# A two-layer graph network on one core: p turned by VectorE and the weights of a tile made in four operations

## The chip, the cores and the metric

The kernel runs on one core of a Trainium2 chip. A core has five engines that run beside each other and meet only at semaphores: TensorE (matrix multiplication; its weight loads are listed apart), VectorE, ScalarE and GpSimd (elementwise work; in the profile DVE, ACT and POOL), and SyncE (SP), which here only issues transfers. POOL issues transfers too. All transfers run on 16 DMA engines. Operands lie in SBUF, 128 partitions wide; matrix products arrive in PSUM, which TensorE writes and VectorE or ScalarE reads.

The metric is the device time of one execution in microseconds, the median of several runs.

## The reference

Sixteen graphs (B) of 1024 nodes (N) with 256 features (D) pass through two layers, each followed by a residual sum and a layer norm. `adj` holds 0 or 1.

Layer 0 takes scores e = leaky(h * a0 @ h^T), a sigmoid where `adj` is 1, and alpha @ h + bias. Layer 1 is an attention whose logits are a sum of a row's and a column's term:

```python
Hh = h @ W
s, d = Hh @ a_src, Hh @ a_dst
e = where(adj != 0, exp(-leaky_relu(s[:, None] + d[None, :], 0.2)), 0)
h_prime = (e @ Hh) / rowsum(e)
x = layernorm(x + elu(h_prime))
```

The exponential of the sum factors. With p = exp(-0.8 s) and q = exp(-0.8 d), and with exp(-0.2 d) put into Hh and what depends on the row alone cancelled by the division, a weight becomes min(p * q, adj): p runs along the columns of a tile (the rows i of the result), q along its partitions (the nodes j that are summed over).

## The kernel before

A batch is 8 tiles of 128 nodes. `adj` lies transposed, so a tile has the summed node j on the partitions and all 1024 rows i on the free axis, in bf16 (`adjs`, two halves of four tiles). The main loop runs over b = 1 to 15 and has three stages, each with a loop of eight steps. The order of the instructions is written out by hand: every engine takes its own in the order of the program, and each waits only for what it reads or overwrites.

1. Strips. For each tile jt of batch b: the scores on TensorE (L227), two tanh on ScalarE (L235, L236), their maximum on VectorE (L237), times `adj` into `al` (`finish`, L243), the diagonal on POOL (L253). The scores are symmetric, so only the upper half is computed: `dump` turns a strip in 32x32 blocks (L259) and stores it (`mir`), `gather` loads it as columns of the lower half of `al`, and `mask` (L274) finishes these. Between the strips TensorE makes Hh of the batch before (`project`, L405), and ScalarE takes from it exp(-0.2 d) (L413), p and q (L414) and Hh (L415). At step 6 `share_p` brings p to all partitions.
2. Sums of layer 0. For each tile t: eight products (L342), then bias and residual (L352), statistics (L295, L297) on VectorE. The weights of layer 1 of the batch before (`weights`, L449) stand among these: none at steps 0 and 1, tiles 0 and 1 at step 2, then 2, 3, 4, 5, and tiles 6 and 7 at step 7, each ahead of that step's L352.
3. Sums of layer 1 of the batch before. For each tile t: eight products of `es` with Hh (L456), which take the weights' tiles in the order 0 to 7; then division and ELU (L479, L480, L488, L489), residual (L494, L496), statistics; beside it x and x1 are turned for the next batch (L191, L381).

The last batch has no next one. Its p is spread without a transfer: TensorE transposes a column that is repeated 128 times (`spread_p`, L424) and ScalarE copies it (L425). Its weights are made while TensorE already multiplies: `weights` 0 before the division of the tile that closes batch 14, 1 to 3 after it, 4 to 7 in a loop over m in which each tile is used for four products at once.

p, before: `project` leaves p and q as pairs, p of tile t in column (t, 0) of `pqs` (three buffers). `share_p` has TensorE transpose the eight columns to 8 rows of 128 (L431), ScalarE copy them (L433), POOL store the 4 KB (L435), wait, and load them back onto all 128 partitions (L437). Both transfers stand in POOL's queue between the diagonals of tiles 6 and 7 (L253). The sums keep their results in three PSUM buffers (`ps_acc`); a transposed p takes one of `ps_t`.

Of the kernel before, what the change touches and what calls it, by code (L numbers as in the profile page):

```python
# [9 lines left out]
F32 = mybir.dt.float32  # L10
# [3 lines left out]
AF = mybir.ActivationFunctionType  # L14
ALU = mybir.AluOpType
# [3 lines left out]
P = 128  # L19
HALF = 512  # L20
BIG = 1.0e30
SLOPE = 0.2
SQ = 32
# [7 lines left out]
def one_kind_pass(  # L31
# [33 lines left out]
    nc = tc.nc  # L65
    B, N, D = x.shape
    NT = N // P
    ND = D // P
    HT = HALF // P
# [4 lines left out]
    const = ctx.enter_context(tc.tile_pool(name="const", bufs=1))  # L74
    four = ctx.enter_context(tc.tile_pool(name="four", bufs=4))
    one = ctx.enter_context(tc.tile_pool(name="one", bufs=1))
    two = ctx.enter_context(tc.tile_pool(name="two", bufs=2))
    dram = ctx.enter_context(tc.tile_pool(name="dram", bufs=2, space=bass.MemoryType.DRAM))
    small = ctx.enter_context(tc.tile_pool(name="small", bufs=3))
    ps_e = ctx.enter_context(tc.tile_pool(name="ps_e", bufs=3, space=PSUM))  # L80
    ps_t = ctx.enter_context(tc.tile_pool(name="ps_t", bufs=2, space=PSUM))
# [5 lines left out]
    xs, adjs = {}, {}  # L87
# [56 lines left out]
    ident = const.tile([P, P], F32, tag="ident", name="ident")  # L144
# [20 lines left out]
    pcol = ps_e.tile([P, HALF], F32, tag="e", name="pcol")[:, 0:ND]  # L165
    nc.tensor.transpose(pcol, arow, ident[0:ND, 0:ND])
    nc.scalar.copy(acol, pcol)
    power = const.tile([P, NT], F32, tag="power", name="power")
    nc.gpsimd.memset(power, -0.5)
    def make_Wx(c):  # L170
# [191 lines left out]
    x1Ts, Hs, pqs, p_bcs, es = {}, {}, {}, {}, {}  # L362
# [28 lines left out]
    def project(b, t):  # L391

        if t == 0:
            if b < B - 1:
                H = one.tile([P, NT, D + 1], F32, tag="H", name=f"H_{b}")
                Hs[b] = [H[:, m, :] for m in range(NT)]
            else:
                Hs[b] = []
                for g in range(2):
                    H = two.tile([P, HT, D + 1], F32, tag=f"adj{g}", name=f"H_{b}_{g}")  # L400
                    Hs[b] += [H[:, m, :] for m in range(HT)]
            pqs[b] = small.tile([P, NT, 2], F32, tag="pq", name=f"pq_{b}")
        pt = ps_acc.tile([P, D + 2], F32, tag="acc", name=f"pH_{b}_{t}")
        for c in range(ND):
            nc.tensor.matmul(  # L405
                pt,
                lhsT=x1Ts[b][:, c, ts(t, P)],
                rhs=Wx[:, c, :],
                start=(c == 0),
                stop=(c == ND - 1),  # L410
            )
        w = Hs[b][t][:, D : D + 1]
        nc.scalar.activation(w, pt[:, 1:2], AF.Exp, scale=-SLOPE)  # L413
        nc.scalar.activation(pqs[b][:, t, :], pt[:, 0:2], AF.Exp, scale=SLOPE - 1.0)  # L414
        nc.scalar.mul(Hs[b][t][:, 0:D], pt[:, 2:], w)  # L415

    def spread_p(b, g):

        if g == 0:
            p_bcs[b] = one.tile([P, N], F32, tag="p", name=f"p_{b}")  # L420
        pt = ps_t.tile([P, HT, P], F32, tag="t", name=f"pp_{b}_{g}")
        for t in range(HT):
            col = pqs[b][:, g * HT + t, 0:1]
            nc.tensor.transpose(pt[:, t, :], col.to_broadcast([P, P]), ident)  # L424
        nc.scalar.copy(p_bcs[b][:, ts(g, HALF)], pt.rearrange("p t q -> p (t q)"))  # L425

    def share_p(b):


        pt = ps_t.tile([P, HT, P], F32, tag="t", name=f"prow_{b}")[0:NT, 0, :]  # L430
        nc.tensor.transpose(pt, pqs[b][:, :, 0], ident)  # L431
        row = one.tile([NT, P], F32, tag="row", name=f"row_{b}")
        nc.scalar.copy(row, pt)  # L433
        p_row = dram.tile([N], F32, tag="p_row", name=f"p_row_{b}")
        nc.gpsimd.dma_start(p_row.rearrange("(t p) -> t p", p=P), row)  # L435
        p_bcs[b] = one.tile([P, N], F32, tag="p", name=f"p_{b}")
        nc.gpsimd.dma_start(p_bcs[b], p_row.partition_broadcast(P))  # L437

    def check_pq(b):
        near = small.tile([P, NT, 2], F32, tag="near", name=f"near_{b}")  # L440
        nc.vector.tensor_scalar(near, pqs[b], LOW, 1.0 / LOW, ALU.max, ALU.min)
        nc.vector.tensor_tensor(near, near, pqs[b], ALU.is_equal)
        nc.vector.tensor_reduce(fit[:, b : b + 1], near, AX.XY, ALU.min)

    def weights(b, m):

        if m == 0:
            es[b] = one.tile([P, NT, N], F32, tag="ew" if b < B - 1 else "al", name=f"e_{b}")
        nc.vector.scalar_tensor_tensor(  # L449
            es[b][:, m, :], p_bcs[b], pqs[b][:, m, 1:2], adjs[b, m // HT][:, m % HT, :], ALU.mult, ALU.min  # L450
        )

    hs, ys, y_of, mv1s, r1s = {}, {}, {}, {}, {}

# [108 lines left out]
    for b in range(1, B):  # L563
# [7 lines left out]
        for jt in range(NT):  # L571
            if jt == 4:
                mask(b, 0)
            strip(b, jt)
            if prev == 0 and jt < 2:
                scale0(0, HT + 2 * jt)
                scale0(0, HT + 2 * jt + 1)
            finish(b, jt)
            if jt < NT - 1:
                dump(b, jt)  # L580
            if prev == 0 and jt == 0:
                turn_x1(0, 0)
            if prev == 0 and jt == 2:
                transpose_x1(0)
            if jt >= 1:
                gather(b, jt - 1)
            for t in projects[jt]:
                project(prev, t)
            if jt == 6:
                share_p(prev)  # L590
            if jt >= 6:
                mask(b, jt - 5)
        check_pq(prev)
        if not last:
            load_x(b + 1, [nc.sync])
# [26 lines left out]
        for t in range(NT):  # L622
# [59 lines left out]
    for m in range(NT):  # L682
# [421 lines left out]
def kernel(  # L1104
# [69 lines left out]
```

## Time and profile before

The median is 1272.78 us (1272.75 to 1272.94, three runs).

| | us |
|---|---|
| the profiled execution's own time | 1273.82 |
| its span | 1271.7 |
| TensorE's matmuls busy | 1261.2 (99%) |
| weight loads (beside them) | 1025.7 (81%) |
| VectorE | 924.9 (73%) |
| ScalarE | 651.4 (51%) |
| GpSimd | 293.5 (23%) |
| L449, the weights, 128 x 1269 ns | 159.7 |
| L431, the transpose of p, 15 x 273 ns | 4.1 |
| VectorE's waits for p | 26.1 in 15 |

Times in the profile count from the start of the span. A line of the timeline gives start, duration, engine, line, operation, result and operands, number of instructions, and in brackets how long the engine had been idle and what ended that. Where a line stands for several instructions (x2), its duration runs from the first one's start to the last one's end. A line of the busy times by stretch gives the stretch, its length, then for PE, PEld, DVE, ACT and POOL the busy time and the number of instructions, TensorE's granted clock, the DMA engines' busy share and GB/s.

### The profile page before, as it was taken

How to read it: one execution, taken by the hardware profiler on the slowest of the kernel's cores; microseconds unless marked ns; L12 is line 12 of the kernel's file. 1: busy time of each engine (PE TensorE's matmuls, PEld its weight loads, DVE VectorE, ACT ScalarE, POOL GpSimd, SP SyncE). 2: the span in 40 equal slices, each digit the busy share in tenths (PEclk: the TensorE clock that was granted, in tenths of full speed). 3: DMA queues.
4: the chain of work that ended last, by engine and by line, in shares of the span. 5: the costliest groups of instructions: out<-in, count | busy, mean ns of one | idle time of the engine just before them, and what ended most of it. 6: DMA issues, size and time to landing. Idle time of an engine off the chain costs nothing.

```text
span 1271.7 us, 17514 instructions
## 1 busy us (share of the span) xinstructions
PE 1261.2 (99%) x5484; PEld 1025.7 (81%) x5484; DVE 924.9 (73%) x2017; ACT 651.4 (51%) x1469; POOL 293.5 (23%) x593
## 2 busy tenths in 40 slices
PE   9999999999999999999999999999999999999997
PEld 6788787887878878788787887878788787887886
DVE  5686867858678686786768868687686867868657
ACT  4644645456454564544645445454455645456434
POOL 2213231212312122121232212223112231212203
PEclk9999999999999999999999999999999999999999
DMA  9388595895949869497695966949579595895312
GB/s 219 67 174 143 103 188 96 176 181 101 194 88 180 168 117 200 77 183 154 130 194 92 182 133 139 209 83 182 117 168 188 95 190 97 174 181 103 99 34 69
DMA packets 603416, 180.24 MB, mean 142 GB/s; under 512 B 481722, under 2 KB 585652, under 8 KB 603316
## 3 DMA queue, kind: packets, MB, share of 16 engines
q1 hardware_dynamic: 581760, 135.85, 54.3%
q0 software_dynamic: 20864, 42.53, 18.6%
q8 instruction: 46, 0.75, 0.3%
q10 hardware_dynamic: 692, 0.66, 0.2%
q14 instruction: 54, 0.44, 0.1%
HBM read 151.91 MB, written 60.62 MB: 167 GB/s over the span
## 4 chain that ended last, share of the span: by engine, by line
PE 98%; DMA 1%; DVE 0%; ACT 0%; issue 0%; ACTq 0%; DVEq 0%
PE acc L342 35%; PE acc L456 35%; PE pe L227 19%; PE pH L405 9%; DMA x<-in_x 1%; PE pal L282 0%; PE prow L431 0%; PE pp L424 0%; ACT y L325 0%; ACT y_kept L325 0%; ACT L666 0%; PE px1T L388 0%; DVE y L494 0%; PE pxT L203 0%; ACTq L136 0%
## 5 line engine op out<-in xcount | busy, mean ns | idle before, releaser
L342 PE MATMUL acc<-x,al 128*128 128x256 f32 x2048 | 445.5, 379 | 0.0
L456 PE MATMUL acc<-H,e 128*128 128x257 f32 x2032 | 445.3, 380 | 0.0
L456 PEld LDWEIGHTS acc<-H,e 128*128 128x128 f32 x2032 | 384.8, 190 | 57.2 <-DVE e L449 0.6
L342 PEld LDWEIGHTS acc<-x,al 128*128 128x128 f32 x2048 | 387.7, 190 | 51.7
L227 PE MATMUL pe<-xa,xT 128*128 128x384 f32 (+1 forms) x720 | 250.9, 486 | 0.0
L227 PEld LDWEIGHTS pe<-xa,xT 128*128 128x128 f32 x720 | 132.7, 189 | 80.8 <-issue 43.1
L325 ACT ACTIVATE x<-x,mr,r 128x256 f32<-128x256 f32 x128 | 69.4, 592 | 227.8 <-POOL mr L321 227.8
L449 DVE SCALAR_TENSOR_TENSOR e<-p,pq,adj 128x1024 f32<-128x1024 f32 x128 | 159.7, 1269 | 29.2 <-DMA p<-p_row 26.1
L304 POOL TENSOR_SCALAR ve<-mv 128x4 f32<-128x4 f32 (+2 forms) x49 | 16.8, 343 | 657.0 <-DVE mv L297 652.9
L488 ACT ACTIVATE h<-acc,rinv 128x256 f32<-128x256 f32 x126 | 59.1, 469 | 203.4 <-DVE rinv L480 187.9
L235 ACT ACTIVATE tb<-pe 128x512 f32<-128x512 f32 (+1 forms) x192 | 94.1, 490 | 119.8 <-PE pe L227 94.6
L479 DVE TENSOR_SCALAR rinv<-acc 128x1 f32<-128x1 f32 x127 | 19.9, 157 | 161.2 <-PE acc L456 161.1
L237 DVE TENSOR_TENSOR tb<-tb,low 128x512 f32<-128x512 f32 (+1 forms) x192 | 103.3, 543 | 39.9 <-ACT low L236 39.8
L125 ACT ACTIVATE junk<-adj,minus 128x2048 bf16<-128x2048 bf16 x64 | 127.3, 1989 | 0.0
L405 PE MATMUL pH<-Wx,x1T 128*128 128x258 f32 x512 | 126.3, 381 | 0.0
L405 PEld LDWEIGHTS pH<-Wx,x1T 128*128 128x128 f32 x512 | 97.2, 190 | 35.8 <-issue 14.3
L253 POOL TENSOR_TENSOR al<-ident,al 128x128 f32<-128x128 f32 x128 | 67.0, 523 | 230.4 <-DVE al L243 229.9
L243 DVE SCALAR_TENSOR_TENSOR al<-tb,adj 128x512 f32<-128x512 f32 (+7 forms) x132 | 97.4, 739 | 5.3 <-DVE tb L237 0.4
L236 ACT ACTIVATE low<-pe 128x512 f32<-128x512 f32 (+1 forms) x192 | 93.2, 485 | 0.5 <-DVE tb L237 0.5
L274 DVE SCALAR_TENSOR_TENSOR al<-al,adj 128x512 f32<-128x512 f32 (+3 forms) x150 | 77.3, 539 | 19.7 <-DMA al<-mir 19.6
L352 DVE SCALAR_TENSOR_TENSOR x<-acc,bias_bc 128x256 f32<-128x256 f32 x128 | 53.7, 420 | 41.5 <-PE acc L342 41.5
L259 DVE STREAM_TRANSPOSE tb<-tb 128x896 f32<-128x896 f32 (+6 forms) x105 | 74.7, 712 | 3.6
(108 smaller groups left out, 950.1 us busy)
## 6 DMA issues: line engine op xcount, KB each, us to landing
adj<-in_adjT POOLq DMA_DIRECT2D x30, 1024.0 KB, 10.3
x_rows<-x SPq DMA_DIRECT2D x31, 512.0 KB, 4.6
x1T<-x_rows SPq DMA_DIRECT2D x248, 64.0 KB, 2.5
out<-y_kept SPq DMA_DIRECT2D x30, 512.0 KB, 6.8
x<-in_x SPq DMA_DIRECT2D x14, 1024.0 KB, 6.1
xT<-in_x SPq DMA_DIRECT2D x112, 128.0 KB, 4.7
p<-p_row POOLq DMA_DIRECT2D x15, 512.0 KB, 4.5
mir<-tb SPq DMA_DIRECT2D x60, 112.0 KB, 3.0
```

Of the source, the lines that this page charges most:

```text
L125: nc.scalar.activation(junk, rows, AF.Square, bias=minus1, scale=2.0, accum_out=chk[:, b * CHECKS + n : b * CHECKS + n + 1],)
L227: nc.tensor.matmul(pe[:, 0:w], lhsT=xTs[b][:, c, ts(jt, P)], rhs=xas[b][:, c, ds(jt * P + o, w)], start=(c == 0), stop=(c == ND - 1),)
L235: nc.scalar.activation(tb[:, ds(o, w)], pe[:, 0:w], AF.Tanh, scale=0.5)
L236: nc.scalar.activation(low[:, 0:w], pe[:, 0:w], AF.Tanh, scale=0.5 * SLOPE)
L237: nc.vector.tensor_tensor(tb[:, ds(o, w)], tb[:, ds(o, w)], low[:, 0:w], ALU.max)
L243: nc.vector.scalar_tensor_tensor(als[b][:, jt, c0:c1], tbs[b, jt][:, c0 - jt * P : c1 - jt * P], 1.0, adjs[b, jt // HT][:, jt % HT, c0:c1] ...
L259: nc.vector.transpose(tb, tb)
L274: nc.vector.scalar_tensor_tensor(v, v, 1.0, rows, ALU.add, ALU.mult)
L342: nc.tensor.matmul(acc, lhsT=als[b][:, jt, ts(t, P)], rhs=xs[b][:, jt, :], start=(jt == 0), stop=(jt == NT - 1),)
L405: nc.tensor.matmul(pt, lhsT=x1Ts[b][:, c, ts(t, P)], rhs=Wx[:, c, :], start=(c == 0), stop=(c == ND - 1),)
L449: nc.vector.scalar_tensor_tensor(es[b][:, m, :], p_bcs[b], pqs[b][:, m, 1:2], adjs[b, m // HT][:, m % HT, :], ALU.mult, ALU.min)
L456: nc.tensor.matmul(acc, lhsT=es[b][:, m, ts(t, P)], rhs=Hs[b][m], start=(m == 0), stop=(m == NT - 1),)
```

## The change

p and q are kept apart in one tile `pq_kept`, 128 x 32, cleared once: columns 0 to 7 hold p of the eight tiles, columns 8 to 15 q, the rest zeros. `share_p` turns it in one instruction on VectorE, which transposes each 32x32 block by itself: block i then has p of the nodes 32 i to 32 i + 31 of every tile in its first 8 rows. One DMA stores all 128 rows of 32 numbers (16 KB), and one loads of each of the four blocks its first 8 rows (four runs of 1 KB) onto all partitions. So p lies there as (i, t, j), where it was (t, i, j). The weights of a tile are made in four operations of 8 x 32 elements each, one for each i, whose result and `adj` have 32 neighbouring elements in each tile of columns.

`spread_p` of the last batch writes p in the new order with the same two copies. `check_pq` follows the new shape. Nothing else is moved.

```diff
+    pq_kept = const.tile([P, SQ], F32, tag="pq", name="pq_kept")
+    nc.gpsimd.memset(pq_kept, 0.0)
@@ project
-            pqs[b] = small.tile([P, NT, 2], F32, tag="pq", name=f"pq_{b}")
+            pqs[b] = pq_kept[:, 0 : 2 * NT].rearrange("p (k t) -> p k t", k=2)
-        nc.scalar.activation(pqs[b][:, t, :], pt[:, 0:2], AF.Exp, scale=SLOPE - 1.0)
+        nc.scalar.activation(pqs[b][:, :, t], pt[:, 0:2], AF.Exp, scale=SLOPE - 1.0)
@@ spread_p
-            p_bcs[b] = one.tile([P, N], F32, tag="p", name=f"p_{b}")
+            p_bcs[b] = one.tile([P, P // SQ, NT, SQ], F32, tag="p", name=f"p_{b}")
-            col = pqs[b][:, g * HT + t, 0:1]
+            col = pqs[b][:, 0, ds(g * HT + t, 1)]
-        nc.scalar.copy(p_bcs[b][:, ts(g, HALF)], pt.rearrange("p t q -> p (t q)"))
+        nc.scalar.copy(
+            p_bcs[b].rearrange("p i t j -> p t i j")[:, ts(g, HT), :, :],
+            pt.rearrange("p t (i j) -> p t i j", j=SQ),
+        )
@@ share_p
-        pt = ps_t.tile([P, HT, P], F32, tag="t", name=f"prow_{b}")[0:NT, 0, :]
-        nc.tensor.transpose(pt, pqs[b][:, :, 0], ident)
-        row = one.tile([NT, P], F32, tag="row", name=f"row_{b}")
-        nc.scalar.copy(row, pt)
-        p_row = dram.tile([N], F32, tag="p_row", name=f"p_row_{b}")
-        nc.gpsimd.dma_start(p_row.rearrange("(t p) -> t p", p=P), row)
-        p_bcs[b] = one.tile([P, N], F32, tag="p", name=f"p_{b}")
-        nc.gpsimd.dma_start(p_bcs[b], p_row.partition_broadcast(P))
+        pT = one.tile([P, SQ], F32, tag="pT", name=f"pT_{b}")
+        nc.vector.transpose(pT, pq_kept)
+        p_row = dram.tile([P // SQ, SQ, SQ], F32, tag="p_row", name=f"p_row_{b}")
+        nc.gpsimd.dma_start(p_row.rearrange("i t j -> (i t) j"), pT)
+        p_bcs[b] = one.tile([P, P // SQ, NT, SQ], F32, tag="p", name=f"p_{b}")
+        nc.gpsimd.dma_start(p_bcs[b], p_row[:, 0:NT, :].partition_broadcast(P))
@@ weights
-        nc.vector.scalar_tensor_tensor(
-            es[b][:, m, :], p_bcs[b], pqs[b][:, m, 1:2], adjs[b, m // HT][:, m % HT, :], ALU.mult, ALU.min
-        )
+        e = es[b][:, m, :].rearrange("p (t i j) -> p i t j", i=P // SQ, j=SQ)
+        rows = adjs[b, m // HT][:, m % HT, :].rearrange("p (t i j) -> p i t j", i=P // SQ, j=SQ)
+        for i in range(P // SQ):
+            nc.vector.scalar_tensor_tensor(
+                e[:, i], p_bcs[b][:, i], pqs[b][:, 1, m : m + 1], rows[:, i], ALU.mult, ALU.min
+            )
```

More of the change, by code (lines that the diff above doesn't have):

```diff
@@ L419, in spread_p @@
         if g == 0:
-            p_bcs[b] = one.tile([P, N], F32, tag="p", name=f"p_{b}")
+            p_bcs[b] = one.tile([P, P // SQ, NT, SQ], F32, tag="p", name=f"p_{b}")
         pt = ps_t.tile([P, HT, P], F32, tag="t", name=f"pp_{b}_{g}")
         for t in range(HT):
-            col = pqs[b][:, g * HT + t, 0:1]
+            col = pqs[b][:, 0, ds(g * HT + t, 1)]
             nc.tensor.transpose(pt[:, t, :], col.to_broadcast([P, P]), ident)
-        nc.scalar.copy(p_bcs[b][:, ts(g, HALF)], pt.rearrange("p t q -> p (t q)"))
+        nc.scalar.copy(
+            p_bcs[b].rearrange("p i t j -> p t i j")[:, ts(g, HT), :, :],
+            pt.rearrange("p t (i j) -> p t i j", j=SQ),
+        )
     def share_p(b):
-        pt = ps_t.tile([P, HT, P], F32, tag="t", name=f"prow_{b}")[0:NT, 0, :]
-        nc.tensor.transpose(pt, pqs[b][:, :, 0], ident)
-        row = one.tile([NT, P], F32, tag="row", name=f"row_{b}")
-        nc.scalar.copy(row, pt)
-        p_row = dram.tile([N], F32, tag="p_row", name=f"p_row_{b}")
-        nc.gpsimd.dma_start(p_row.rearrange("(t p) -> t p", p=P), row)
-        p_bcs[b] = one.tile([P, N], F32, tag="p", name=f"p_{b}")
-        nc.gpsimd.dma_start(p_bcs[b], p_row.partition_broadcast(P))
+        pT = one.tile([P, SQ], F32, tag="pT", name=f"pT_{b}")
[4 more added lines that the diff above has]
+        nc.gpsimd.dma_start(p_bcs[b], p_row[:, 0:NT, :].partition_broadcast(P))
     def check_pq(b):
-        near = small.tile([P, NT, 2], F32, tag="near", name=f"near_{b}")
+        near = small.tile([P, 2, NT], F32, tag="near", name=f"near_{b}")
         nc.vector.tensor_scalar(near, pqs[b], LOW, 1.0 / LOW, ALU.max, ALU.min)
```

## The prediction

> **What bounds the kernel now.** The page comes first, for who is full and what the chain that ended last is made of; then the busy time of one batch, cut into its three stages; then the instructions around the change in order of time; then the same at the end of the program, where the last batch has no next one to hide behind.
>
> ```profile
> span 1271.7 us, 17514 instructions
> PE 1261.2 (99%) x5484; PEld 1025.7 (81%) x5484; DVE 924.9 (73%) x2017; ACT 651.4 (51%) x1469; POOL 293.5 (23%) x593
> PE 98%; DMA 1%; DVE 0%; ACT 0%; issue 0%; ACTq 0%; DVEq 0%
> ...
> 624.83:652.46 27.63, 27.63 (x131) 24.34 (x129) 22.50 (x47) 9.79 (x20) 8.80 (x14) 1.00 0.95 174
> 652.46:680.30 27.84, 27.84 (x130) 24.25 (x128) 16.45 (x46) 14.89 (x27) 3.31 (x9) 1.00 0.82 163
> 602.26:624.83 22.57, 22.57 (x82) 14.87 (x81) 19.02 (x34) 15.76 (x48) 6.89 (x13) 1.00 0.56 100
> ```
>
> TensorE never rests, at full clock, in any stage. So only two things can move the time: instructions taken from TensorE, and moments at which it is made to wait. The stage to look at is the first of the three rows, the sums of layer 0, because the weights are made beside it: VectorE is busy 22.50 of 27.63 us there, and its results must be ready when TensorE comes to them.
>
> ```profile
> 624.27 0.27 PE L431 MATMUL prow<-ident,pq 128*8 128x128 f32 x1
> 624.38 0.61 PE L227 MATMUL pe<-xa,xT 128*128 128x128 f32 x4
> ...
> 626.50 0.46 POOL L253 TENSOR_TENSOR al<-ident,al 128x128 f32<-128x128 f32 x1 [0.82 <-DVE al L243]
> 626.89 0.64 POOL L435 DMA_DIRECT2D p_row<-row  x1
> 631.35 0.55 POOL L437 DMA_DIRECT2D p<-p_row  x1 [3.82 <-DMA p_row<-row]
> 636.30 2.48 DVE L449 SCALAR_TENSOR_TENSOR e<-p,pq,adj 128x1024 f32<-128x1024 f32 x2 [2.54 <-DMA p<-p_row]
> 649.21 0.42 DVE L352 SCALAR_TENSOR_TENSOR x<-acc,bias_bc 128x256 f32<-128x256 f32 x1 [1.16 <-PE acc L342]
> 650.23 2.45 DVE L449 SCALAR_TENSOR_TENSOR e<-p,pq,adj 128x1024 f32<-128x1024 f32 x2
> 652.46 3.86 PE L456 MATMUL acc<-H,e 128*128 128x257 f32 x17
> ...
> 1235.58 3.66 DVE L449 SCALAR_TENSOR_TENSOR e<-p,pq,adj 128x1024 f32<-128x1024 f32 x3
> 1244.47 2.45 DVE L449 SCALAR_TENSOR_TENSOR e<-p,pq,adj 128x1024 f32<-128x1024 f32 x2
> ```
>
> Read here that VectorE already waits 2.54 us for p, that its last tile ends at 652.68 while TensorE starts to use the tiles at 652.46, and that two tiles take 2.45 us though one alone has a mean of 1269 ns (the second starts about 0.1 us before the first has ended). The line L456 of the page's groups adds that TensorE's weight load waited for L449 only 0.6 us in the whole run; the list of waits gives it as two waits, 0.3 us each the longest.
>
> **The change part by part.**
>
> TensorE loses the transpose of L431, 15 times. Its record lasts 0.27 us, but the next matmul starts 0.11 us after it, so that is what it occupies: 15 x 0.11 = -1.65 us, on the bounding engine. ScalarE loses L433 (238 ns x15) and a PSUM buffer is not taken; ScalarE is 51% busy, so nothing.
>
> VectorE gains one block transpose of 128x32 per batch. L259 takes 446 ns for 256 columns and 311 for 128, so 32 columns are 0.21 us. It stands behind the transpose at 626.45, when its input has been there since 623.85 (the last exponential to p and q, L414), so it adds no wait; behind it in VectorE's queue are the masks L274, the last strip's maximum, tile 7 and its check, and the first sum's end, and VectorE idles 2.54 us before the weights. Hidden; without that idle time it would cost 0.21 per batch, 3 us in all.
>
> p's way to its tile. POOL's queue is as before: the first DMA waited for its turn behind L253 at 626.50, not for `row` (ready at 625.26), so taking TensorE and ScalarE out of the way gains nothing; the new transpose ends at about 626.95: +0.1. The store grows from 4 KB in 8 rows to 16 KB in 128 rows of 128 B. Nearest rows: `p_row<-row` lands in 3.1 us, the 16 KB stores `mir<-tb` in 3.5 and the 32 KB ones in 2.4: -0.2 to +0.4, taken 0.2. POOL takes 0.64 and 0.55 us to issue p's two DMAs and 0.85 for L102's (more and larger rows): 0 to +0.3 for the second, taken 0.2. The broadcast moves the same 512 KB in pieces of 1 KB instead of 4 KB: `p<-p_row` lands in 4.5 us, `x_rows<-x`, as many bytes in pieces of 1 KB, in 4.6, `out<-y_kept`, the same shape under more traffic, in 6.8. So 0 to +1.5 for the busy queues, taken 0.3, nearer to 4.6. p lands s = +0.8 us later (-0.1 to +2.3). The second DMA still waits in POOL's queue for the first; behind it is only tile 7's L253 (631.92), which TensorE needs some 20 us later. SP's queue is not touched.
>
> The weights: 512 instructions of 256 elements for 128 of 1024, with the same number of elements. L243, the same operation, takes 424 ns for 256, 689 for 512 and 1225 for 1024: 1.043 ns an element, 1.07 us per 1024. Start to start, L449 takes 3.66 less 1.27 over two, 1.19 us: each instruction adds 0.12. Three more per tile: d = 3 x 0.12 = +0.36 us. Bounds: L274's 128 and 512 columns take 0.89 us together where the second alone has 0.70, so 0.06 more than the elements need, d = 0.18; and if the four pieces did not overlap at all, as the dependent chain L352, L295 does with 0.46 us per 256 elements, 4 x 0.46 - 1.19, d = 0.65. I take 0.36, since the row is the same line. A wait between the four isn't likely: they write different columns, and the gathers L267 write columns of the same `al` while L243 goes on writing its rows.
>
> [...]
>
> Does that reach TensorE? In the steady batch VectorE works 652.68 - 636.30 - 1.16 = 15.22 us from p's landing to the last tile; now 15.22 + 8 x 0.36 = 18.1. TensorE needs the last tile 14 matmuls of 0.2175 (27.84/128) after 652.46, its load 0.2 earlier: 2.85 us after the first L456. In the 15 batches p landed 18.6 to 16.2 us before that matmul, 17.1 on average (two at 16.2, two at 16.6). So the last tile ends -17.1 + 0.8 + 18.1 = 1.8 us after it, 1.0 before it is needed; in the worst batches 0.1 before. VectorE's idle 1.16 and 2.6 us of slack pay for it. Late next are the sums' ends behind the first two tiles (L352 at 638.70): they become 640.2 and free a buffer that TensorE wants at 642.1. I put 0.15 us in all for the tight batches. A stall sets in when 8d + s passes 3.7 in the worst batches and 4.7 in the average one; each batch then pays its own excess.
>
> At the end of the program nothing covers it. From 1235.58 VectorE makes seven tiles (two residual sums between) to 1246.92, and TensorE takes the last at 1231.62 + 72 x 0.2175 + 0.33 of waits, load 0.2 earlier: 1247.4. Seven times 0.36 is 2.5, less 0.5 of slack: +2.0 us (0.8 to 4.05), fully on the path.
>
> Edits at nothing: the one memset of the kept tile on POOL (L169, a like one, 0.23 us; POOL then idles 10 us); exponentials written 8 apart (L414, 174 ns, ScalarE idle half the time); the two spread copies (L425, 585 ns: the second is followed by a tile that has 1.5 us to spare before 1235.31); one kept p/q tile instead of three buffers (rewritten 32 us after its last reader, 22 in the last batch).
>
> Sum: -1.65 + 2.0 + 0.15 = +0.5 us. The profiled execution took 1273.82, the median is 1272.78, 0.1% below; so 1274.3 under the profiler and 1273.3 in the median.
>
> **The rivals.** Time differences of 0.2%, 2.5 us, are about what a measurement of this kernel tells from no change.
>
> 1. Forecast, 0.56: VectorE's 46 us more (128 x 0.36) are hidden in every batch but the end. From d = 0.18, -1.65 + 0.8 = -0.85, to d = 0.42 with s = 1.0, where 8d + s = 4.4 and the four tightest batches pay 0.6, 0.6, 0.2 and 0.2: -1.65 + 2.45 + 1.6 = +2.4. Its own range is 1271.9 to 1275.2.
>
> 2. Slower, 0.20: the pieces don't overlap and VectorE bounds the sums' stage. At d = 0.65, 8d + s = 6.0, 1.3 us past 4.7 in each of 14 batches: 18 + 4.05 - 1.65 = +20.4, 1293. At d = 0.5 the tight half of the batches pays some 4 us: 4 + 3 - 1.65, 1278. It decides from d = 0.45. For it: runs of 32 elements in three dimensions stand nowhere in the trace. Against: L449's own pairs overlap.
>
> 3. Slower, 0.16: p lands late because 512 small packets on POOL's queue share engines that are 95% busy in this stage. At s = 2.3: 2.9 + 2.3 - 4.7 = 0.5, 14 times 7 us, + 0.35: 1280. It decides from s = 1.6. Against it: 4.6 for `x_rows<-x`.
>
> 4. Faster, 0.05: the transpose cost TensorE its whole 0.27 us, 15 x 0.27 = 4.05, and the tail only 0.8: -3.2, 1269.6. Against: the next matmul starts after 0.11.
>
> The remaining 0.03 I leave open. Faster 0.06, same 0.55, slower 0.39. The range 1271.6 to 1283 leaves out the faster case and the upper half of the second.
>
> **What the profile of the changed kernel would show.** No L431; L456 directly after the sums with no wait for the weights beyond the end of the program; groups of four pieces of about 0.39 us start to start, 1.55 us a tile; the wait for p up from 26.1 us to about 35; the last tile at about 1249.4, and there one TensorE wait of some 2 us. Wrong if TensorE waits for the weights once in each batch, if the pieces are 0.46 apart, or if p lands over 1.6 us later.

## The result and the profile after

The changed kernel takes 1278.34 us in the median (1276.34 to 1282.49, seven runs), the kernel before, on the same chip, 1272.75 (1272.17 to 1274.69, seven runs). The ratio is 1.0049 with a 95% interval of 1.0039 to 1.006: 5.6 us slower, and with a wider spread. The forecast was 1273.3, within 0.2% of no change; its range, 1271.6 to 1283.0, holds the time, its likeliest case does not.

The page of the changed kernel, from its first lines, its chain of waits (shares by engine), its groups and its transfers. A group's line has busy time, mean of one in ns, and after the bar the idle time before it and what ended most of that; a transfer's line ends with the median time from issue to landing.

```profile
span 1275.5 us, 17902 instructions
PE 1261.6 (99%) x5469; PEld 1024.2 (80%) x5469; DVE 966.7 (76%) x2416; ACT 649.0 (51%) x1454; POOL 271.3 (21%) x594
PE 69%; DVE 10%; DMA 5%; issue 1%; ACT 1%; SPq 1%; POOL 0%; DVEq 0%; ACTq 0%; POOLq 0%
...
L464 PE MATMUL acc<-H,e 128*128 128x257 f32 x2032 | 447.5, 380 | 3.8 <-DVE e L457 3.8
...
L457 DVE SCALAR_TENSOR_TENSOR e<-p,pq_kept,adj 128x256 f32<-128x256 f32 x512 | 209.3, 476 | 55.2 <-DMA p<-p_row 52.1
...
p<-p_row POOLq DMA_DIRECT2D x15, 512.0 KB, 6.1
```

Lines have moved: L456 is now L464, L449 is L457, L352 is L355, the two transfers of p are L440 and L442. TensorE does 15 matmuls less and is as busy as before, but the chain that ended last is no longer TensorE's own: VectorE has 10% and the DMA engines 5% of it. The broadcast of p lands 6.1 us after its issue, 4.5 before, and VectorE waits 52.1 us for it, 26.1 before. TensorE's weight loads for L464 now wait 7.9 us for the weights, 0.6 before.

Batch 3 shows how. The timeline of the changed kernel around the point where its sums of layer 1 begin:

```profile
235.16 0.17 DVE L438 STREAM_TRANSPOSE pT<-pq_kept 128x32 f32<-128x32 f32 x1
235.62 0.63 POOL L440 DMA_DIRECT2D p_row<-pT  x1 [0.20 <-issue]
238.98 0.78 POOL L442 DMA_DIRECT2D p<-p_row  x1 [2.72 <-DMA p_row<-pT]
246.84 3.25 DVE L457 SCALAR_TENSOR_TENSOR e<-p,pq_kept,adj 128x256 f32<-128x256 f32 x8 [5.08 <-DMA p<-p_row]
...
250.48 10.23 PEld L345 LDWEIGHTS acc<-x,al 128*128 128x128 f32 x48 [0.35 <-DVE x L355]
251.33 1.66 DVE L457 SCALAR_TENSOR_TENSOR e<-p,pq_kept,adj 128x256 f32<-128x256 f32 x4
...
260.95 3.29 PE L464 MATMUL acc<-H,e 128*128 128x257 f32 x14
261.84 3.23 DVE L457 SCALAR_TENSOR_TENSOR e<-p,pq_kept,adj 128x256 f32<-128x256 f32 x8
265.12 3.09 PE L464 MATMUL acc<-H,e 128*128 128x257 f32 x13 [0.88 <-DVE e L457]
```

The read is issued at 238.98 and the first weights start at 246.84, 7.86 us later. That is 14.11 us before TensorE's first product of the sums of layer 1 (260.95); before, it was 17.1 on average. The last two tiles (261.84) end at 265.07, 4.12 after that product and not within the 2.85 that TensorE allows, so it makes 14 matmuls and waits 0.88 us (1.05 to the next matmul's start, over the usual 0.2175). A smaller second loss stands earlier: the first two tiles push back a sum's end (L355), which frees a PSUM buffer 0.35 us late for the weight load.

All 15 batches follow that rule. In the eight where the first weights start 15.54 us or more before the first product, the last tile ends by 2.69 and TensorE does not wait. In the seven where they start 15.27 or less before it, the last tile ends 2.96 to 4.12 after it and TensorE loses 0.1 to 1.2 us. These losses add up to 3.9 us. The mean of the 15 starts is 15.45, so p is 1.7 us later than before.

At the end of the program, by the timeline (the lines that answer to 1235.58 and 1244.47 of before, and TensorE's):

```profile
1235.93 4.82 DVE L457 SCALAR_TENSOR_TENSOR e<-p,pq_kept,adj 128x256 f32<-128x256 f32 x12
1237.64 5.47 PE L464 MATMUL acc<-H,e 128*128 128x257 f32 x24 [0.28 <-DVE e L457]
...
1243.84 3.74 PE L464 MATMUL acc<-H,e 128*128 128x257 f32 x16 [0.73 <-DVE e L457]
1246.76 3.23 DVE L457 SCALAR_TENSOR_TENSOR e<-p,pq_kept,adj 128x256 f32<-128x256 f32 x8
1248.45 10.70 PE L464 MATMUL acc<-H,e 128*128 128x257 f32 x48 [0.88 <-DVE e L457]
```

Twelve pieces take 4.82 us, so they start 0.396 us apart (4.82 less one of 0.47, over 11) and a tile takes 1.58 us; d is 0.39. TensorE waits three times, 2.4 us from matmul to matmul, where it lost 0.15 before: +2.2, and 0.1 more in the matmuls right behind the waits.

The account of the two profiled executions, whose spans differ by 3.8 us: -1.7 because a batch without waits has a period of 77.93 us and had 78.04; +3.9 in the seven batches; +2.3 at the end; +1.1 between the last matmul and the end of the span (9.0 us, 7.9 before); and -1.9 at the start, where the profiled execution of before happened to wait longer for `x`. Without that last accident, which has nothing to do with the change, it is +5.6, as the medians have it.

### The profile page after: what moved, and what is told of

It is laid out like the page before. It is cut to its first block, busy times and chain, and to the rows that moved or that the text cites. A ratio compares the mean times of both kernels' runs of the same rounds, so it can differ in the third digit from the quotient of the medians.

```text
span 1275.5 us, 17902 instructions
## 1 busy us (share of the span) xinstructions
PE 1261.6 (99%) x5469; PEld 1024.2 (80%) x5469; DVE 966.7 (76%) x2416; ACT 649.0 (51%) x1454; POOL 271.3 (21%) x594
## 4 chain that ended last, share of the span: by engine, by line
PE 69%; DVE 10%; DMA 5%; issue 1%; ACT 1%; SPq 1%; POOL 0%; DVEq 0%; ACTq 0%; POOLq 0%
PE acc L464 30%; PE acc L345 19%; PE pe L230 13%; PE pH L408 6%; DVE e L457 6%; DMA p<-p_row 3%; DMA mir<-tb 1%; DMA p_row<-pT 1%; DVE st L298 1%; DMA al<-mir 1%; DVE al L246 1%; DVE x L355 1%; DVE tb L240 1%; SPq L266 1%; DVE al L277 0%
## 5 line engine op out<-in xcount | busy, mean ns | idle before, releaser
L464 PE MATMUL acc<-H,e 128*128 128x257 f32 x2032 | 447.5, 380 | 3.8 <-DVE e L457 3.8
L345 PE MATMUL acc<-x,al 128*128 128x256 f32 x2048 | 445.7, 379 | 0.0
L464 PEld LDWEIGHTS acc<-H,e 128*128 128x128 f32 x2032 | 384.2, 190 | 63.8 <-DVE e L457 7.9
L345 PEld LDWEIGHTS acc<-x,al 128*128 128x128 f32 x2048 | 387.4, 190 | 52.1 <-DVE x L355 0.3
L457 DVE SCALAR_TENSOR_TENSOR e<-p,pq_kept,adj 128x256 f32<-128x256 f32 x512 | 209.3, 476 | 55.2 <-DMA p<-p_row 52.1
L256 POOL TENSOR_TENSOR al<-ident,al 128x128 f32<-128x128 f32 x128 | 64.4, 504 | 223.9 <-DVE al L246 223.6
L277 DVE SCALAR_TENSOR_TENSOR al<-al,adj 128x512 f32<-128x512 f32 (+3 forms) x150 | 74.1, 518 | 19.5 <-DMA al<-mir 19.4
L328 ACT ACTIVATE y_kept<-y_kept,mr,r 128x256 f32<-128x256 f32 x120 | 64.8, 592 | 1.1 <-DVE y L502 1.1
```

The costliest lines, as they stand in the source:

```text
L328: nc.scalar.activation(y, y, AF.Identity, bias=mr, scale=r)
L345: nc.tensor.matmul(acc, lhsT=als[b][:, jt, ts(t, P)], rhs=xs[b][:, jt, :], start=(jt == 0), stop=(jt == NT - 1),)
L457: nc.vector.scalar_tensor_tensor(e[:, i], p_bcs[b][:, i], pqs[b][:, 1, m : m + 1], rows[:, i], ALU.mult, ALU.min)
L464: nc.tensor.matmul(acc, lhsT=es[b][:, m, ts(t, P)], rhs=Hs[b][m], start=(m == 0), stop=(m == NT - 1),)
```

## The experiments

Ten kernels ran, in three groups, each beside the kernel before on the same chip. That took 1272.43 (33 runs), 1272.55 and 1272.33 us (15 runs each).

| run | what it has | us (lowest to highest) | ratio, 95% interval |
|---|---|---|---|
| pieces alone | p as before, four pieces | 1275.19 (1274.25 to 1275.69) | 1.0020, 1.0011 to 1.0029 |
| turn alone | turn, one 4 KB run, whole tiles | 1271.56 (1270.88 to 1273.67) | 0.9995, 0.9986 to 1.0004 |
| turn and pieces | turn, one 4 KB run, four pieces | 1274.19 (1273.21 to 1277.97) | 1.0017, 1.0007 to 1.0026 |
| last batch whole | the change, batch 15 in whole tiles | 1275.50 (1273.83 to 1279.18) | 1.0027, 1.0018 to 1.0036 |
| late p alone | the change's route, whole tiles | 1271.97 (1271.10 to 1275.23) | 0.9993, 0.9983 to 1.0003 |
| eight runs | turn, p read in eight runs, whole tiles | 1320.89 (1314.90 to 1328.11) | 1.0395, 1.0364 to 1.0427 |
| eight pieces | turn, one 4 KB run, eight pieces | 1328.21 (1323.12 to 1330.98) | 1.0434, 1.0408 to 1.0460 |
| the change again | the change | 1280.34 (1278.83 to 1284.42) | 1.0057, 1.0043 to 1.0071 |
| clear by VectorE | turn alone, kept tile cleared by VectorE | 1271.26 (1271.03 to 1272.32) | 0.9991, 0.9982 to 1.0000 |
| store by SP | turn alone, p's store issued by SP | 1356.19 (1350.69 to 1362.10) | 1.0669, 1.0648 to 1.0691 |

### Pieces alone

The first question is whether four operations a tile are enough to make TensorE wait. This kernel has p's old route and layout, and takes it in pieces.

```diff
-        nc.vector.scalar_tensor_tensor(
-            es[b][:, m, :], p_bcs[b], pqs[b][:, m, 1:2], adjs[b, m // HT][:, m % HT, :], ALU.mult, ALU.min
-        )
+        e = es[b][:, m, :].rearrange("p (t i j) -> p i t j", i=P // SQ, j=SQ)
+        rows = adjs[b, m // HT][:, m % HT, :].rearrange("p (t i j) -> p i t j", i=P // SQ, j=SQ)
+        pv = p_bcs[b].rearrange("p (t i j) -> p i t j", i=P // SQ, j=SQ)
+        for i in range(P // SQ):
+            nc.vector.scalar_tensor_tensor(
+                e[:, i], pv[:, i], pqs[b][:, m, 1:2], rows[:, i], ALU.mult, ALU.min
+            )
```

> The kernel before, with p on its old way (TensorE, 4 KB read in one run) and only the weights made in four pieces of 8 x 32. Theory: a batch stalls only when the pieces' extra work and a late p together pass the slack (8d + s over 3.7 us in the tight batches, 4.7 in the average one). Here 8 x 0.39 = 3.1 and s = 0, so no batch stalls and only the end of the program pays, 7 x 0.39 - 0.5 = 2.2 us: 1275.0, 1.0017. Rival A, the pieces alone make VectorE the bound: TensorE waits for L449's successor in most batches, 4 us or more beside the end: 1279, 1.005. Rival B, the late p alone does it: as the theory here, 1275.

It is 2.8 us slower than before. The list of waits of this kernel (engine and line, who released it; us in total, times, longest) and the line of its transfer:

```profile
DVE e L453 <- DMA p<-p_row: 23.6, 14, 2.6
PEld acc L460 <- DVE e L453: 3.1, 3, 1.3
PE acc L460 <- DVE e L453: 1.9, 3, 0.9
p<-p_row POOLq DMA_DIRECT2D x15, 512.0 KB, 4.4
```

Three waits, all at the end of the program; every batch keeps its period of 78.04 us (from the first product of its sums of layer 1 to the next batch's), and the last tile never ends later than 2.14 us after the first product. So the pieces by themselves cost the end and nothing else. From the last batch's first product of layer 1 to the last matmul of the program this kernel needs 67.41 us and the kernel before 65.10, so the trace has 2.3 of the 2.8; the rest is within the interval, which runs from 1.4 to 3.7 us.

### The turn alone

The change without the pieces: the kept tile, the turn and the larger store stay, but the store writes p in its old order (t, i, j), so that it is read as one run of 4 KB and a tile needs one operation.

```diff
-        nc.tensor.transpose(pt, pqs[b][:, :, 0], ident)
-        nc.scalar.copy(row, pt)
-        nc.gpsimd.dma_start(p_row.rearrange("(t p) -> t p", p=P), row)
-        nc.gpsimd.dma_start(p_bcs[b], p_row.partition_broadcast(P))
+        pT = one.tile([P, SQ], F32, tag="pT", name=f"pT_{b}")
+        nc.vector.transpose(pT, pq_kept)
+        p_row = dram.tile([SQ, P // SQ, SQ], F32, tag="p_row", name=f"p_row_{b}")
+        nc.gpsimd.dma_start(p_row.rearrange("t i j -> i t j"), pT)
+        nc.gpsimd.dma_start(p_bcs[b], p_row[0:NT].rearrange("t i j -> (t i j)").partition_broadcast(P))
```

> p turned by VectorE and stored by one DMA, but written to DRAM in the order (t, i, j), so that the read is one run of 4 KB for each partition and a tile is one operation again. Theory: TensorE is spared 15 x 0.11 us, nothing else is on the path: -1.65 us, 1271.1, 0.9987; p lands 0 to 0.3 us later than before. If the transpose cost TensorE its whole record of 0.27 us: -4, 1268.7. If the turn on VectorE or the store of 16 KB costs time by itself: 1272.8 or more.

0.9 us are saved, and the interval reaches from -1.8 to +0.5. The period of all batches is 77.93, so the trace shows the -1.65 of the transpose in full; but from the last matmul to the end of the span there are 8.7 us and not 7.9. That takes 0.8 back and leaves -0.85, beside the -0.87 of the medians. Where the 0.8 comes from is asked again below.

### Turn and pieces, with p early

The change, but with the order (t, i, j) in DRAM, so that p is read as one run of 4 KB as before.

```diff
-        p_row = dram.tile([P // SQ, SQ, SQ], F32, tag="p_row", name=f"p_row_{b}")
-        nc.gpsimd.dma_start(p_row.rearrange("i t j -> (i t) j"), pT)
-        nc.gpsimd.dma_start(p_bcs[b], p_row[:, 0:NT, :].partition_broadcast(P))
+        p_row = dram.tile([SQ, P // SQ, SQ], F32, tag="p_row", name=f"p_row_{b}")
+        nc.gpsimd.dma_start(p_row.rearrange("t i j -> i t j"), pT)
+        nc.gpsimd.dma_start(p_bcs[b], p_row[0:NT].rearrange("t i j -> (t i j)").partition_broadcast(P))
```

> The changed kernel, with the store in the order (t, i, j), so that p is read in one run of 4 KB and not in four of 1 KB; the weights stay in four pieces. Theory: the four runs are what makes p 1.7 us late; here s is 0 to 0.3, 8d + s = 3.1 to 3.4, under 3.7, no batch stalls: -1.65 + 2.2 = +0.6, 1273.3, 1.0004. If it is the turn, the larger store or the queue that makes p late: first tile again 1.7 us later and 1278, 1.0044. Rival A: 1277 or more whatever p does.

1274.19, 4.15 us less than the change, for nothing but another order in DRAM. Its waits and its transfer:

```profile
DVE e L454 <- DMA p<-p_row: 29.8, 14, 3.3
PEld acc L461 <- DVE e L454: 3.1, 3, 1.3
PE acc L461 <- DVE e L454: 1.9, 3, 0.9
p<-p_row POOLq DMA_DIRECT2D x15, 512.0 KB, 4.4
```

The 3.9 us of the batches are gone, the end is as in the first run. The records of the packets say why p was late. A broadcast is 128 packets of 4 KB, one to each partition, here, before and in the change, and not the 512 small ones of the third rival. The median of a batch's packets is 156 to 196 ns before, and 256 to 448 ns in the change, where the 4 KB of a packet are gathered from four runs of 1 KB that lie 4 KB apart. The store is not to blame: in the change its 128 rows leave as 16 packets of 1 KB and land 3.2 us after their issue, the 8 rows of before 3.1.

### The last batch in whole tiles

```diff
+        if b == B - 1:
+            nc.vector.scalar_tensor_tensor(
+                es[b][:, m, :], p_bcs[b], pqs[b][:, 1, m : m + 1], adjs[b, m // HT][:, m % HT, :], ALU.mult, ALU.min
+            )
+            return
```

(with `spread_p` in the old order again)

> The changed kernel, with batch 15 alone as before: p in the old order and one operation for a tile, so the end of the program is as before while the batches before it stay as changed. Theory: the end's share comes back, 2.2 us (1.9 to 2.7): 1276.1, 1.0027. If the end cost nothing: 1278.3. If the end were the whole loss: 1271.1.

1275.50 against 1278.34: the end is worth 2.8 us by the medians, as in the first run and a little beyond the 1.9 to 2.7 that were expected. The batches' losses stay, between 0.1 and 1.2 us in those where p is late.

### Late p alone

The other corner of the square: p as late as in the change, and whole tiles.

```diff
-        for i in range(P // SQ):
-            nc.vector.scalar_tensor_tensor(
-                e[:, i], p_bcs[b][:, i], pqs[b][:, 1, m : m + 1], rows[:, i], ALU.mult, ALU.min
-            )
+        nc.vector.scalar_tensor_tensor(
+            es[b][:, m, :], p_bcs[b].rearrange("p i t j -> p (i t j)"), pqs[b][:, 1, m : m + 1], adjs[b, m // HT][:, m % HT, :], ALU.mult, ALU.min
+        )
```

> The changed kernel's whole route of p, late landing included, but one operation of 1024 elements per tile: it takes p as it lies, (i, t, j), against columns in the order (t, i, j), so the weights have p in a wrong order of columns; the amount and the kind of the work are those of the kernel before. Theory (p's lateness and the pieces must come together): p lands 5.9 to 6.2 us after its issue, VectorE waits for it some 50 us in all, but 8d + s is only about 1.7, under 3.7, so TensorE waits for no weights in any batch; the end is as before. 1271.6 us, as the second run's 0.9995. Rival B (the late p stalls TensorE by itself): the 4 us of the batches stay, 1275.5, with TensorE's waits for the weights in about 7 of 15 batches.

```profile
DVE e L454 <- DMA p<-p_row: 58.4, 15, 5.7
PEld acc L461 <- DVE e L454: 0.6, 2, 0.3
PEld acc L345 <- DVE x L355: 0.3, 1, 0.3
p<-p_row POOLq DMA_DIRECT2D x15, 512.0 KB, 6.2
```

VectorE waits 58.4 us for p, more than in the change, and TensorE does not notice: 1271.97, as with p early. p is 2.2 us late on average and 3.8 in the worst batch (first weights 13.33 us before the first product instead of 17.1). That batch is the only one with a loss, 0.2 us, in a sum of layer 0, where TensorE waits for a PSUM buffer (L345 for L355). It is not a wait for weights: the last tile ends no later than 1.79 us after the first product, inside the 2.85. So the prediction's point of 3.7 for the worst batches, which is one for the weights, was not reached here, and that it lies so near to 3.8 proves nothing.

So in the batches neither half does it alone. Against the turn alone (1271.56), late p costs 0.4 us, the pieces cost 2.6, all at the end, and both together 6.8: 3.8 us are due to their meeting, on one queue, with one slack of 4.7 us. They did not all run on one chip; by their ratios to the kernel before beside them the meeting is worth 4.3.

### Eight runs

p read in eight runs of 512 B, whole tiles.

```diff
-        p_row = dram.tile([SQ, P // SQ, SQ], F32, tag="p_row", name=f"p_row_{b}")
-        nc.gpsimd.dma_start(p_row.rearrange("t i j -> i t j"), pT)
-        nc.gpsimd.dma_start(p_bcs[b], p_row[0:NT].rearrange("t i j -> (t i j)").partition_broadcast(P))
+        p_row = dram.tile([SQ, 8, P // SQ, SQ], F32, tag="p_row", name=f"p_row_{b}")
+        nc.gpsimd.dma_start(p_row[:, 0].rearrange("t i j -> i t j"), pT)
+        nc.gpsimd.dma_start(p_bcs[b].rearrange("p (t q) -> p t q", q=P), p_row[0:NT, 0].rearrange("t i j -> t (i j)").partition_broadcast(P))
```

> The second run (turn on VectorE, one operation per tile) with p's rows 4 KB apart in DRAM, so that the 4 KB of a partition are read in eight runs of 512 B. Theory (a packet's time grows with the number of runs it is read in, from 159 ns for one run to 300 for four, about 47 ns a run): packets of about 490 ns, p lands about 8 us after its issue, s about 3.5 us, which with whole tiles is just at the point (3.7) where the worst batches begin to wait: 1271.6 to 1273. Rival C (the packets were slow for another reason, the order of the blocks or a busier moment): packets of 159 ns, or 300 as with four runs, landing 4.4 or 6.1, and 1271.6 us in either case.

Rival C falls, for more runs did make the packets slower; the theory's size was too small: packets took 606 to 852 ns in the median of a batch, not 490, p landed after 10.0 us, not 8, and the kernel took 1320.89. From batch 6, by the timeline:

```profile
487.69 0.92 POOL L439 DMA_DIRECT2D p<-p_row  x1 [3.60 <-DMA p_row<-pT]
...
499.00 2.48 DVE L451 SCALAR_TENSOR_TENSOR e<-p,pq_kept,adj 128x1024 f32<-128x1024 f32 x2 [9.46 <-DMA p<-p_row]
501.40 0.42 DVE L355 SCALAR_TENSOR_TENSOR x<-acc,bias_bc 128x256 f32<-128x256 f32 x1
501.87 11.69 PEld L345 LDWEIGHTS acc<-x,al 128*128 128x128 f32 x48 [3.95 <-DVE x L355]
501.87 12.09 PE L345 MATMUL acc<-x,al 128*128 128x256 f32 x48 [3.55 <-DVE x L355]
```

Here it is not the weights that TensorE waits for, though they are what is late. In VectorE's order the sum's end (L355, 501.40) stands behind the first two tiles (499.00), so the wait of 9.46 us for p holds it up, and TensorE waits 3.55 us for the PSUM buffer that it frees, in the sums of layer 0. The 14 periods lose 1.0 to 5.7 us each, 39.8 in all.

Not all of that is waiting. Behind four of the waits, of 3.0 to 4.0 us, TensorE's granted clock was 0.5 for 3.41 us; behind one of 3.3 us and the shorter ones it was not. The wait shown is one of the four. By stretches (the clock is the third number from the end):

```profile
498.10:501.50 3.40, 0.22 (x2) 0.00 (x0) 2.50 (x3) 0.00 (x0) 0.00 (x0) 0.99 0.93 236
501.50:504.90 3.40, 3.03 (x7) 2.49 (x8) 3.26 (x8) 0.00 (x0) 0.00 (x0) 0.50 0.79 108
504.90:508.30 3.40, 3.40 (x17) 3.00 (x17) 3.33 (x7) 0.00 (x0) 3.03 (x3) 1.00 1.27 153
```

TensorE runs 7 matmuls there and 17 in the next stretch. Half of 3.41 is 1.7 us, so by this estimate up to 6.8 of the 39.8 us are the clock's. The rest is the wait itself: late p does cost by itself, from beyond the point that the run before just touched.

### Eight pieces

The turn with p early, and pieces of 128 elements. With g the order of the loop is i, then halves of the tile's columns (pv is p in that view).

```diff
         for i in range(P // SQ):
-            nc.vector.scalar_tensor_tensor(
-                e[:, i], p_bcs[b].rearrange("p (t i j) -> p i t j", i=P // SQ, j=SQ)[:, i], pqs[b][:, 1, m : m + 1], rows[:, i], ALU.mult, ALU.min
-            )
+            for g in range(2):
+                nc.vector.scalar_tensor_tensor(
+                    e[:, i, ts(g, HT)], pv[:, i, ts(g, HT)], pqs[b][:, 1, m : m + 1], rows[:, i, ts(g, HT)], ALU.mult, ALU.min
+                )
```

> The third run (turn on VectorE, p early in one run of 4 KB) with eight pieces of 128 elements per tile in place of four of 256. Theory: a piece is 0.133 us for its elements and 0.129 more, as measured (0.396 less 0.267), so 2.10 us a tile, d = 0.91 and 8d = 7.3; the last tile then ends 4.6 to 6.9 us after the first product that takes the weights, which is 1.8 to 4.1 later than TensorE wants it: about 3 us in each of 15 batches, 45 us, and about 5.9 at the end of the program. 1322 us (1300 to 1335), ratio 1.039. Rival D (VectorE has more room than the last tile's time says, since its other work moves aside): only the end pays, 1278 us, ratio 1.004.

1328.21, within the expected range. Its waits, and two of its lines from batch 15:

```profile
PEld acc L463 <- DVE e L456: 50.2, 35, 2.4
PE acc L463 <- DVE e L456: 35.8, 31, 2.0
```
```profile
1238.35 2.16 DVE L456 SCALAR_TENSOR_TENSOR e<-p,pq_kept,adj 128x128 f32<-128x128 f32 x8
...
1241.43 4.26 DVE L456 SCALAR_TENSOR_TENSOR e<-p,pq_kept,adj 128x128 f32<-128x128 f32 x16
```

Eight more pieces add 4.26 - 2.16 = 2.10 us, as worked out from the four. Every batch now waits for weights; 14 periods lose 44.2 us. In five of them the clock was 0.5 for 3.41 us behind the waits, so by the estimate above some 8 us are the clock's and about 36 the waits': that the 45 us expected for the waits look right is in part luck. With one cause at twice its size the threshold is crossed in each batch, so the small loss of the change was not a constant price of its pieces but the part of 8d + s that stuck out.

### The change again

> The changed kernel itself, beside the others on one chip. 1277.5 us (1276.3 to 1279), ratio 1.004: of it 2.2 us at the end and about 4 in the batches; the first of these runs should differ from it by both, some 6 us.

1280.34, beyond the upper figure expected, 1279, and 8.4 us above the run with late p and whole tiles where some 6 were expected. Its profiled execution, with a span of 1282.3 us, lost 8.7 us in the 14 periods where the first had lost 3.7. It is the same program; by the first execution, a batch in which p lands a few tenths later pays for it (0.1 to 1.2 us in seven batches), and one in which it lands earlier gains nothing (no wait in the other eight). Two of its waits:

```profile
PE acc L464 <- DVE e L457: 6.0, 8, 0.9
PE acc L345 <- DVE x L355: 2.4, 3, 1.4
```

So there are two places to pay. In the first execution the sums of layer 1, which wait for the weights, had nearly all of the loss. Here the sums of layer 0 have 3.5 of the 8.7 us: as in the run with eight runs, the end of a sum stands behind the first two tiles and frees its PSUM buffer late. In the first execution that wait stands only in the batch with the latest p, batch 3 (0.35 us), and it holds back the first product too: in neither execution do the first weights start less than 14.11 us before it, and no batch loses more than 1.2 us to the last tile.

That fits the wider spread of the changed kernel's times, 6.2 us in the seven runs shown first where the kernel before had 2.5; but in the later groups the kernel before spread by 4.2 to 5.9 us through single long runs, so the spread alone shows little.

### Who ends the program

In the turn alone, 0.8 us were lost after the last matmul. POOL closes the program with an INC_SWDGE_SEM and a DRAIN, and the records of the trace have these durations in ns:

```
                         INC_SWDGE_SEM   DRAIN
before, pieces alone               712    2192
the change and all runs
  with its turn, but:          936-940    3094
eight runs                         440    1052
store by SP                        580    1624
```

In the changed kernel POOL ends its DRAIN at 1274.66 and reaches the closing barrier at 1274.71, while SyncE's last step ahead of it was over at 1273.92 and the barrier lets all go at 1274.84; before, POOL was done at 1269.58 and waited for the others until 1270.94. So POOL has become the last. Two edits of the turn-alone kernel ask whether the one instruction more on POOL or the store in its queue does it.

```diff
-    nc.gpsimd.memset(pq_kept, 0.0)
+    nc.vector.memset(pq_kept, 0.0)
```

> The second run (turn on VectorE, one operation per tile) with the kept tile cleared by VectorE in place of POOL. In every run with the turned p so far POOL's closing instructions after its last work are longer than before (INC_SWDGE_SEM 0.94 us against 0.71, the DRAIN behind it 3.09 against 2.19), and POOL is the last at the closing barrier. Theory E (the store of 128 rows in POOL's queue is what lengthens them): the same as the second run, 0.94 and 3.09, and 1271.6 us, 0.9995. Theory F (the one more instruction on POOL shifts its program): back to 0.71 and 2.19, the end 0.7 us earlier, 1270.9, 0.9988.

The closing instructions stay at 936 and 3094 ns, so the one instruction more is not what lengthens them: that half of theory F falls. Its other half holds in this trace. POOL starts them 2.91 us after the last matmul, 2.81 before and 3.74 in the turn alone; it is through at 6.98 and no longer last, since SyncE's last step ends at 7.21, and the barrier lets the engines go at 7.35 and not at 7.98. What is won is lost elsewhere: VectorE, which now has the instruction more, ends 1.2 us behind all others. So the clearing on POOL had delayed its closing by 0.8 us, beside what lengthens it. The time, 1271.26, is that of the turn alone within the noise.

```diff
-        nc.gpsimd.dma_start(p_row.rearrange("t i j -> i t j"), pT)
+        nc.sync.dma_start(p_row.rearrange("t i j -> i t j"), pT)
```

> The second run with p's store issued by SP in place of POOL. Theory E (the store in POOL's queue lengthens POOL's closing): back to 0.71 and 2.19 us, the end 0.7 us earlier, and in the batches nothing changes as long as SP, which now waits for the turn between its own transfers, is not late with the gathers: 1270.9 us, 0.9988. Theory F: POOL's closing stays at 0.94 and 3.09, 1271.6, 0.9995. If SP's wait delays the gathers, VectorE's masks wait longer for them and p comes no earlier; a stall of TensorE would show as a wait in the strips.

The closing gets shorter, to 580 and 1624, even less than before. So their length changed with what POOL's queue was given (3094 ns with the store, 1624 without), but not simply by the size of the store: eight runs, with a store of as many rows, has the shortest, 1052. How it follows stays open. And the time went the other way, 84 us up:

```profile
330.66 0.17 DVE L435 STREAM_TRANSPOSE pT<-pq_kept 128x32 f32<-128x32 f32 x1
...
336.59 0.53 SPq L437 DMA_DIRECT2D p_row<-pT  x1
337.31 0.34 SPq L270 DMA_DIRECT2D al<-mir  x1
...
338.23 10.94 SPq L117 DMA_DIRECT2D xT<-in_x  x8
339.26 0.64 POOL L439 DMA_DIRECT2D p<-p_row  x1 [8.32 <-DMA p_row<-pT]
```

SyncE issues the store 5.8 us after the turn, since it issues 11 dumps and gathers of the strips in between, and the read then runs beside the loads of `x`: it lands after 7.2 us though it is one run of 4 KB. Its packets take 183 ns in the median, little more than the 159 of before; that the loads are what delays it was not tried. From the turn to the first weights there are 15.8 us in this batch, 11.7 in batch 3 of the change. As in the run with eight runs TensorE waits for PSUM buffers, 48.4 us in 15 waits, and behind 13 of them the clock was 0.5, for 58.0 us in all: by the same estimate up to 29 us of the loss. SyncE's own wait did not hurt the gathers, as had been feared; being behind them hurt p.

## Why the prediction was right and where it failed

**The step that failed is p's way to its tile, s.** It was put at +0.8 us and is +1.7 by the starts of the first tile. Inside it the broadcast was taken as +0.3, nearer to `x_rows<-x` (4.6 us, pieces of 1 KB) than to the upper bound of +1.5; the medians say 4.5 to 6.1, +1.6, at the far end of the bound and just past it. The row chosen as nearest was no likeness: a packet of 4 KB that was put together from four runs took nearly twice as long as one from a single run (305 ns against 159, each the middle one of the 15 batches' medians), and the trace of before has the 159 ns of the latter only. The turn (0.17 us, 0.21 predicted), the store (POOL waited 41.7 us for it in 14 batches, 45.1 before) and the read's issue (0.78 us, 0.55 before, +0.2 taken) came out as said.

**The point was right.** The prediction let a stall set in when 8d + s passes 3.7 us in the worst batches and 4.7 in the average one, and let the third rival, p late, decide from s = 1.6. With d = 0.39 the average point is at s = 4.7 - 3.1 = 1.6, and s was 1.7: nearly half of the batches stuck out. The 0.15 us put in for tight batches became 3.9 in one profiled execution and some 10 in another. (By the prediction's own figures the worst batches' point is 16.2 + 2.85 - 15.22 = 3.8.) The second place to pay, a buffer freed late behind the first two tiles, was named there too, and taken to cost next to nothing: it has 0.2 us of the first execution's loss and 3.5 of the second's. What happened is the third rival's late p, through longer packets and not more of them, at its very threshold: it had 7 us for the batches at s = 2.3. So the range holds the time because this rival was let into it; the forecast, that all but the end is hidden, failed. The runs with late p alone, with turn and pieces, and with eight pieces show that it takes the sum of both terms.

**d** was 0.36 and is 0.39, well below the 0.45 from which the second rival decides; pieces alone make no batch wait, so that rival falls. The pieces of 256 elements start 396 ns apart and last 476, those of 128 start 262 apart and last 344: neighbours overlap by about 80 ns, where the prediction read about 0.1 us from a pair of L449.

**The transpose of TensorE**: -0.11 us in every batch's period (78.04 to 77.93), exactly as read from the start of the next matmul and not from the record's 0.27. The fourth rival falls with it.

**The end**: +2.0 predicted, 2.3 by the trace, 2.6 to 2.8 by pairs of medians.

**Not in the sum at all**: POOL's closing. The prediction did not look at the stretch from the last matmul to the end of the span. In both profiled executions of the change, and in the five other runs that have its turn, clear the tile on POOL and show the DRAIN of 3094 ns, this stretch is 0.8 to 1.1 us longer than before, and POOL comes to the barrier 0.5 to 0.9 us after SyncE. It eats half of what the transpose saved.

The edits at nothing were worth next to nothing: no wait of TensorE in any run answers to the clearing, the exponentials or the single kept tile; with the clearing on POOL its closing starts 3.74 us after the last matmul, without it 2.91.

## What to carry to other kernels

When two small costs fall on one queue with slack ahead of a bounding engine, add them before comparing with the slack, and compare with the tightest repetition rather than the mean: in the batches each was free alone (no wait from the pieces, 0.2 us from late p) and the sum was not (3.9 us), and close to the point one program's two profiled executions lost 3.7 and 8.7 us in the same 14 periods. What this broadcast cost depended on how the bytes of one partition lie in DRAM (4.3 to 4.5 us from one run with the store on POOL, 6.1 to 6.2 from four, 10.0 from eight), so arrange the layout on the store, where 128 rows landed in 3.2 us and 8 in 3.1, and read one run. Look also at what stands after the last matmul: of the 1.65 us saved on TensorE, POOL's closing took back 0.8 in the turn alone.

The best version found is the turn with one 4 KB run and whole tiles. It came out at 0.9995 and, cleared by VectorE, at 0.9991, with intervals that reach 1.0004 and 1.0000: not shown to be faster than the kernel before.

## What the runs showed of the hardware that was not expected

- A 4 KB packet of p's broadcast took 159 ns from one run in DRAM, some 300 to 360 from four runs of 1 KB (three executions) and about 720 from eight of 512 B, each 4 KB apart. From four to eight runs the distance stays and the time doubles, so here their number or length counts; whether the distance does too was not tried.
- The change's store of 128 rows of 128 B into contiguous DRAM left as 16 packets of 1 KB in each of the 15 batches.
- In the weights, an operation of 256 elements with a mean duration of 476 ns let the next one start after 396; 128 elements, 344 and 262.
- POOL's closing DRAIN took 2.19 us before and with the pieces alone, 3.09 in the change, 1.62 with p's store issued by SP and 1.05 with eight runs, and in the changed kernel it was the last thing that the program waited for. With one clearing less on POOL its closing started 0.8 us sooner (2.91 us after the last matmul, 3.74 with it).
- In the run with the store by SP, 14 of TensorE's waits took 2.5 to 4.2 us, and behind 13 of them its granted clock was 0.5 for 3.41 us or twice that; behind the waits of the change, up to 1.4 us, it was not.
